# A graph layer's kernel: one more group of rows gathered from x, and another order around the last two groups of edges

## The chip, the cores and the metric

The kernel runs on one core of a Trainium2 chip. The metric is device time in microseconds (us). The engines are TensorE (PE: matmuls; PEld: its weight loads), VectorE (DVE), ScalarE (ACT), GpSimd (POOL) and SyncE (SP). In this kernel POOL issues the gathers (indirect DMAs), and SP nearly all other transfers.

## The reference

N = 6250 nodes with H = 128 features, E = 100000 edges with 4 attributes, the edges sorted by destination:

```python
msg_in = jnp.concatenate([node_features[src], node_features[dst], edge_features], axis=1)
h = jax.nn.silu(msg_in @ mW1 + mb1)
messages = h @ mW2 + mb2
aggregated = jax.ops.segment_sum(messages, dst, num_segments=N)
upd_in = jnp.concatenate([node_features, aggregated], axis=1)
u = jax.nn.silu(upd_in @ uW1 + ub1)
updated = u @ uW2 + ub2
return layer_norm(node_features + updated, ln_g, ln_b)
```

The result is `layernorm(x + that)`, so each node's row is normed twice. All is in float32.

## The kernel before

**Tables.** A product of a gathered row with a weight is the same as a gathered row of the product. So the kernel first forms two tables in device memory: `tab_a` = x times the first 128 rows of `mW1`, and `tab_b` = x times the second 128 rows plus the bias. For that, x is turned tile by tile on TensorE (L339), multiplied (L377), copied out by ACT and DVE (L379, L380) and written by SP (L383, L384), in parts of eight tiles (L367).

**Groups of edges.** The edges go in 98 groups of 1024, each eight tiles of 128 (the last has six). `fetch(g)` (L273) issues eight gathers on POOL, one for each tile, into one of six buffers named `ga`. For groups below `RAW` = 5 it gathers rows of x itself, so that POOL needn't wait for `tab_a`; for the others rows of `tab_a`. Its further arguments are TensorE instructions that the gathers wait for: with two of them, the first holds gather 0 of the group and the second gather 4 (L285 to L294). The groups gathered from x have to be turned (`turn_rows`, L357: eight transposes and a copy back into the buffer) so that `products` can multiply them by the first part of `mW1` (L626). All groups of x are turned while the tables are made. Group 5 is fetched at L404, from `tab_a`, after the turn of group 2.

**The loop** (L680) takes one group in each turn. For group g:

- SP loads the rows of `tab_b` that belong to the group's 96 destinations (`mv`) and the attributes (`st`), four groups ahead (L591, L592).
- `hidden(g)`: DVE adds the gathered rows and the product from PSUM (L640; groups below `RAW` don't need this add), then ACT takes the Silu into `h` (L641).
- `products(g + 2)`: TensorE spreads `tab_b` and the attributes over the edges (L623), and for groups below `RAW` adds the product of the turned rows (L626).
- `node_matrix(g + 3)` (L596) and `edge_matrix(g + 1)` (L609, `oh`) build one-hot matrices on DVE.
- `add(g - 2)` (L665; every fourth group with the counts, L670) adds the sums of an earlier group to `acc`.
- `by_nodes(g)`: TensorE sums `h` over the destinations (L652).
- A fetch: from `CLOSE` = 14 on `fetch(g + 2, begun[g + 2], summing[g])`; that is, gather 0 waits for the first matmul of the group's own products, and gather 4 for the first matmul of the sums of the group now worked on. `products(0)` at L677 stands ahead of the loop, and group 6 takes buffer 0 of the gathers, which `products(0)` reads.

**Nodes.** When the sums of four tiles of nodes are complete, a generator `node_batch` (L466) does the update and both norms, in pieces that end at a `yield`; `advance` (L569) runs one piece of each batch under way, in the loop one a turn, two in turns 92 to 94 and four from turn 95 on (L721). A batch's pieces are: load of its rows `xs`; the products with `u1x`, the fused bias and the sums (L510, L511, L515); Silu to `uT` (L518); the products with `u2` (L521, L530); adding `xs` and the moments (L532, L483, L484); the square root on ACT (L489); scaling (L539 to L546) and second moments; the second root; the shift; the final scaling on ACT (L560); the store by SP. The batch next to last has the tiles from 44 (three tiles) and is started in turn 95. The last batch, `final`, has two tiles and takes its buffers from the gathers' pool.

**After the loop** (L724 to L757) stand what remains of batch 44, the load of `final`'s rows, an activation of one element that brings in the Silu table (L748), the add of group 96, the add and Silu of group 97 in two pieces (L732, L733), its sums, and the rest of `final`.

**Order.** The order on each engine is the order in which the program text issues (`manual_schedule`); each engine's instructions wait on others by semaphores. Two side jobs run as generators too: `destination_checks` (L230), started in turn 2, and `fuse_weights` (L450), started in turn 8. Both use the PSUM tile `y` (`node_y`, L422) that the node batches use, of which there is one.

Of the kernel before, what the change touches and what calls it, by code (L numbers as in the profile page):

```python
# [8 lines left out]
F32 = mybir.dt.float32  # L9
# [9 lines left out]
P = 128  # L19
# [5 lines left out]
def kernel(  # L25
# [40 lines left out]
    nc = tc.nc  # L66
# [5 lines left out]
    G = 8  # L72
# [6 lines left out]
    RB = 14  # L79
    CLOSE = 14  # L80
    LEAD = 4
    RAW = 5
    MADE = 3
    NQ = 4
    NM = 5
# [141 lines left out]
        nc.vector.tensor_copy(base_f, row)  # L227
        nc.vector.tensor_copy(base_i, row)

    def destination_checks(pm):  # L230

        nc.tensor.matmul(pm[:, 0, :NG], ones[0:1, :], base_f, start=True, stop=True)
        yield
        yield
        nc.vector.tensor_scalar(base_p, pm[:, 0, :NG], p_col, None, op0=OP.add)

        far = work.tile([P, 2], F32, name="far", bufs=1)
        nc.vector.tensor_reduce(far[:, 0:1], rel, AX.XY, OP.max)
        nc.vector.tensor_reduce(far[:, 1:2], rel, AX.XY, OP.min)
        mid = (W - 1) / 2  # L240
        nc.vector.tensor_scalar(far, far, -mid, None, op0=OP.add)
        nc.vector.tensor_mul(far, far, far)
        nc.vector.tensor_reduce(far[:, 0:1], far, AX.X, OP.max)
        farthest = work.tile([1, 1], F32, name="farthest", bufs=1)
        yield
        nc.tensor.transpose(pm[0:1, 1, :], far[:, 0:1], ident)
        yield
        yield
        nc.vector.tensor_reduce(farthest, pm[0:1, 1, :], AX.X, OP.max)
        bad = work.tile([1, 2], F32, name="bad", bufs=1)  # L250
        nc.vector.tensor_scalar(bad[:, 0:1], farthest, mid * mid, None, op0=OP.is_gt)

        below = work.tile([1, NG], F32, name="below", bufs=1)
        nc.vector.memset(below, 0.0)
        for i0, n, g in batches[:-1]:
            nc.vector.memset(below[:, g:], float((i0 + n) * P))
        nc.vector.tensor_sub(below, below, base_f)
        nc.vector.tensor_reduce(bad[:, 1:2], below, AX.X, OP.max)
        nc.vector.scalar_tensor_tensor(
            bad_i, bad[:, 1:2], 0.0, bad[:, 0:1], op0=OP.is_gt, op1=OP.max  # L260
        )
# [95 lines left out]
    def turn_rows(g):  # L357
# [4 lines left out]
        nc.vector.tensor_copy(rows[g], px)  # L362
        return ins

    turn_x(*parts[0])
    fetch(1)
    for k, (i0, n) in enumerate(parts):  # L367
# [31 lines left out]
        if k == 4:  # L399
# [1 line left out]
            destinations(0)  # L401
            load_bases(0)
            turn_rows(1)
    fetch(RAW, None, turn_rows(2))  # L404
    for g in range(3, RAW):
        turn_rows(g)
    if E < NG * GE:
        pad = tpool.tile([ED, NG * GE - E], F32, name="pad")
# [13 lines left out]
    def node_y():  # L422
        return node_ps.tile([P, BT, H], F32, name="y")
# [42 lines left out]
    def node_batch(i0, n, work, new, y, final=False):  # L466

        cols = slice(i0 * P, (i0 + n) * P)
        m = (min((i0 + n) * P, N) - i0 * P) // n
        assert m * n == min((i0 + n) * P, N) - i0 * P  # L470

        def rows_of(t):

            return t[i0 * P : i0 * P + m * n].rearrange("(p j) f -> p j f", j=n)

        def flat(t):
            return t[:, :n].rearrange("p i f -> p (i f)")

        def moments(v):
            mv = work.tile([P, BT, 2], F32, name="mv", bufs=2)  # L480
            for i in range(n):
                st = work.tile([P, 6], F32, name="st", bufs=2)
                nc.vector.bn_stats(st, v[:, i, :])  # L483
                nc.vector.bn_aggr(mv[:, i, :], st)  # L484
            return mv

        def std(mv):
            r = work.tile([P, BT], F32, name="r", bufs=2)
            nc.scalar.activation(r[:, :n], mv[:, :n, 1], AF.Sqrt, bias=eps)  # L489
            return r  # L490

        xs = new("xs")
        if m < P:
            nc.vector.memset(xs[m // 32 * 32 :, :n], 0.0)
        nc.sync.dma_start(xs[:m, :n], rows_of(x))
        sums, counts = acc[:, cols], deg[:, cols]
        if not final:

            acc_b, deg_b = new("acc_b"), new("deg_b", DR)
            nc.scalar.copy(flat(acc_b), sums)  # L500
            nc.scalar.copy(flat(deg_b), counts)
            sums, counts = flat(acc_b), flat(deg_b)
        yield
        xb = xs
        if final:
            xb = new("xb")
            nc.vector.tensor_add(xb[:, :n], xs[:, :n], b_b[:, None, :].to_broadcast([P, n, H]))
            nc.vector.tensor_add(xs[:, :n], xs[:, :n], ub2_b[:, None, :].to_broadcast([P, n, H]))
        y = y()
        nc.tensor.matmul(flat(y), u1x, xT[:, cols], start=True, stop=False)  # L510
        nc.tensor.matmul(flat(y), mb2u, counts, start=False, stop=False)  # L511
        if final:

            yield
        nc.tensor.matmul(flat(y), w2u, sums, start=False, stop=True)  # L515
        yield
        uT = new("uT")
        nc.scalar.activation(flat(uT), flat(y), AF.Silu, bias=ub1_col)  # L518
        yield
        if not final:  # L520
            nc.tensor.matmul(  # L521
                y[:, :n],
                ones[0:1, :],
                ub2_row[:, None, :].to_broadcast([1, n, H]),
                start=True,
                stop=False,
            )
        by_p = flat(uT).rearrange("k (p j) -> k p j", j=n)
        for i in range(n):
            nc.tensor.matmul(y[:, i, :], by_p[:, :, i], u2, start=final, stop=final or i == n - 1)  # L530
        yield
        nc.vector.tensor_add(y[:, :n], y[:, :n], xs[:, :n])  # L532
        mv = moments(y)
        if not final:
            nc.vector.tensor_add(xs[:, :n], xs[:, :n], b_b[:, None, :].to_broadcast([P, n, H]))
        yield
        r = std(mv)
        yield
        nc.vector.reciprocal(r[:, :n], r[:, :n])  # L539
        z = new("z")  # L540
        for i in range(n):
            nc.vector.scalar_tensor_tensor(
                y[:, i, :], y[:, i, :], mv[:, i, 0:1], g_b, op0=OP.subtract, op1=OP.mult
            )
            nc.vector.scalar_tensor_tensor(
                z[:, i, :], y[:, i, :], r[:, i : i + 1], xb[:, i, :], op0=OP.mult, op1=OP.add  # L546
            )
        mz = moments(z)
        yield
        rz = std(mz)  # L550
        yield
        nc.vector.reciprocal(rz[:, :n], rz[:, :n])
        shift = work.tile([P, BT], F32, name="shift", bufs=2)
        nc.vector.scalar_tensor_tensor(
            shift[:, :n], mz[:, :n, 0], -1.0, rz[:, :n], op0=OP.mult, op1=OP.mult
        )
        yield
        o = z
        for i in range(n):
            nc.scalar.activation(  # L560
                o[:, i, :], z[:, i, :], AF.Identity, bias=shift[:, i : i + 1], scale=rz[:, i : i + 1]
            )
        yield
        (nc.scalar if final else nc.sync).dma_start(rows_of(out), o[:m, :n])
# [115 lines left out]
    for g in range(NG):  # L680
        if g == 1:
            load_weights()
        if g == 2:
            running.append(destination_checks(node_y()))
        if g == 8:
            running.append(fuse_weights())
        for c in range(1, NC):
            if g == max(1, c * EC // GE - 10):
                attributes(c)
            if g == max(1, c * EC // GE - 10) + 1:  # L690
                attribute_rows(c)
        if g + LEAD < NG:
            load(g + LEAD)
        last = g >= NG - 1
        if not last:
            h[g] = hidden(g)
        if g + 2 < NG:
            pre[g + 2] = products(g + 2)
        if g + MADE < NG:
# [5 lines left out]
        if last:  # L705
            break
        pt[g] = by_nodes(g, h.pop(g), oh.pop(g))
        if CLOSE <= g + 2 < NG:
            fetch(g + 2, begun[g + 2], summing[g])
        elif g == 0:  # L710
            fetch(7, ended[1], begun[2])
        elif g == 1:
            fetch(8, begun[3], summing[1])
        elif g % 2:
            fetch(g // 2 + 8, ended[g + 1], begun[g + 2] if g == CLOSE - 3 else ended[g + 2])
        if g >= NG - 3:
            add(g - 1, pt.pop(g - 1))
        for i0, n, first in batches[:-1]:
            if g == (first if first >= NG - 3 else first + 1):
                running.append(node_batch(i0, n, *node_tiles(nodes, node_y)))  # L720
        for _ in range(4 if g >= NG - 3 else 2 if g >= NG - 6 else 1):  # L721
            advance(running)

    g = NG - 1  # L724
    n = tiles_of(g)
    ga, pg, oh_g, h_g = rows.pop(g), pre.pop(g), oh.pop(g), hbuf[g % NH]
    s = work.tile([P, G, H], F32, name="s")
    primed = consts.tile([1, 1], F32, name="primed")
    before = running.pop()

    def piece(lo, hi):
# [1 line left out]
        nc.scalar.activation(h_g[:, lo:hi], s[:, lo:hi], AF.Silu)  # L733
        sums(g, pt[g], h_g, oh_g, lo, hi)

    final = node_batch(
        *batches[-1][:2],
        nodes,

        lambda name, p=P: gath.tile([P, G, H], F32, name="ga")[:p, :BT],  # L740
        lambda: rows_ps()[:, :BT],
        final=True,
    )
    while running:
        advance(running)
    next(final)

    nc.scalar.activation(primed, ones[0:1, 0:1], AF.Silu)  # L748
    add(g - 1, pt.pop(g - 1))
    pt[g] = degrees(g)  # L750
    next(final)
# [165 lines left out]
```

## Time and profile before

| what | us |
| --- | --- |
| median of 3 runs | 1178.11 (1177.94 to 1178.4) |
| the profiled execution | 1179.78 |
| its span in the trace | 1177.7 |
| mean granted clock of TensorE | 0.668 of full |
| POOL, 782 gathers at 0.95 us and other work | 743.2 busy |

The profile is one execution; its times are compared with its own 1179.78, not with the median. Two rows of the page's groups are for the two kinds of gathers:

```profile
L277 POOL DMA_INDIRECT ga<-tab_a,src_i x742 | 703.7, 948 | 384.2 <-issue 187.1
...
L277 POOL DMA_INDIRECT ga<-in_x_dram,src_i x32 | 30.7, 960 | 16.4 <-issue 8.8
```

A row gives the line, the engine, the operation, output and input, the count, the busy time, the mean in ns, and the idle time just before with what ended most of it. A line of the timeline gives start, duration, engine, line, operation and, in brackets, how long the engine had been idle and what ended that. "issue" is time in which the engine waited for nothing that the profile shows. "remote" means a releaser that the trace couldn't name.

### The profile page before, as it was taken

The numbers are of one execution on the slowest core, as the hardware profiler recorded it, in microseconds if no ns is written. First come the engines' busy times: TensorE is split into PE (matmuls) and PEld (weight loads), VectorE is DVE, ScalarE is ACT, GpSimd is POOL, SyncE is SP. The second block draws the span as 40 slices with busy tenths as digits, with TensorE's granted clock in tenths as the row PEclk, the third lists the DMA queues.
The fourth block names the chain that finished last, engine by engine and source line by source line (L and its number), as shares of the span: only waits on it lengthen the run. The fifth ranks groups of instructions, "written<-read, shape, count | busy, mean of one in ns | idle before, by whom it ended". The sixth has DMA issues, their size and how long they took to land.

```text
span 1177.7 us, 11313 instructions
## 1 busy us (share of the span) xinstructions
PE 747.7 (63%) x3645; PEld 675.3 (57%) x3645; DVE 486.4 (41%) x1017; ACT 238.9 (20%) x297; POOL 743.2 (63%) x790
## 2 busy tenths in 40 slices
PE   5776896656756666567647666656566565656654
PEld 4575786555655656465646565555565464656533
DVE  4461654433532523532533353342343252353344
ACT  2211121220321311120221121121132131122132
POOL 6646666665666666666666666666666666656660
PEclk9877877676565666567566667666666667667665
DMA  8762232222222221222222213221222222212110
GB/s 198 203 156 71 75 85 65 67 82 61 74 66 73 67 72 52 79 72 73 55 72 76 58 57 81 65 81 56 71 74 66 71 74 63 65 55 69 47 59 20
DMA packets 70076, 89.01 MB, mean 76 GB/s; under 512 B 20703, under 2 KB 51694, under 8 KB 70010
## 3 DMA queue, kind: packets, MB, share of 16 engines
q0 software_dynamic: 25024, 51.30, 15.8%
q1 hardware_dynamic: 40408, 35.03, 10.3%
q10 hardware_dynamic: 4578, 1.89, 0.7%
q8 instruction: 31, 0.51, 0.2%
q14 instruction: 35, 0.29, 0.1%
HBM read 76.78 MB, written 11.38 MB: 75 GB/s over the span
## 4 chain that ended last, share of the span: by engine, by line
PE 35%; issue 32%; POOL 20%; DVE 2%; DMA 1%; another core or an unknown queue 1%; ACT 1%; DVEq 0%; POOLq 0%; SPq 0%; ACTq 0%
POOL ga L277 20%; PE pre L623 17%; PE pt L652 14%; PE pre L626 1%; PE y L530 1%; DMA ga<-tab_a,src_i 1%; PE y L521 1%; PE y L510 1%; PE y L511 0%; PE y L515 0%; DVE s L640 0%; DVE st L483 0%; DVE oh L609 0%; PE pt L647 0%
## 5 line engine op out<-in xcount | busy, mean ns | idle before, releaser
L277 POOL DMA_INDIRECT ga<-tab_a,src_i x742 | 703.7, 948 | 384.2 <-issue 187.1
L623 PE MATMUL pre<-mv,st 100*128 100x128 f32 x1564 | 345.1, 396 | 229.5 <-issue 199.5
L623 PEld LDWEIGHTS pre<-mv,st 100*128 100x128 f32 x1564 | 315.2, 301 | 248.4 <-issue 224.3
L652 PE MATMUL pt<-oh,h 128*128 128x96 f32 x1564 | 293.7, 348 | 147.6 <-issue 143.8
L652 PEld LDWEIGHTS pt<-oh,h 128*128 128x128 f32 x1564 | 279.9, 266 | 165.8 <-issue 162.3
L640 DVE TENSOR_TENSOR s<-ga,pre 128x1024 f32<-128x1024 f32 x92 | 112.2, 1220 | 502.6 <-DMA ga<-tab_a,src_i 419.8
L641 ACT ACTIVATE h<-s 128x1024 f32<-128x1024 f32 x92 | 97.1, 1056 | 671.5 <-issue 409.6
L596 DVE TENSOR_SCALAR_CACHE_REDUCE st<-near,p_next 96x1024 f32<-96x1024 uint8 x98 | 124.3, 1270 | 2.9 <-DMA near<-near_d 1.5
L609 DVE TENSOR_TENSOR oh<-w_row,rel 128x768 f32<-128x768 f32 x98 | 93.0, 949 | 42.5 <-remote 42.2
L277 POOL DMA_INDIRECT ga<-in_x_dram,src_i x32 | 30.7, 960 | 16.4 <-issue 8.8
L532 DVE TENSOR_TENSOR y<-y,xs 128x512 f32<-128x512 f32 (+1 forms) x12 | 8.3, 688 | 74.4 <-issue 70.7
L641 ACT ACT_TABLE_LOAD x23 | 29.5, 1283 | 24.2 <-PE pre L626 17.6
L489 ACT ACT_TABLE_LOAD x24 | 30.8, 1283 | 6.1 <-DVE st L483 5.7
L377 PE MATMUL wide<-w,xT 128*128 128x256 f32 x98 | 27.6, 441 | 3.5 <-DVE x_sb L380 3.5
L665 DVE TENSOR_TENSOR acc<-acc,pt 128x96 f32 x98 | 23.7, 242 | 12.5 <-PE pt L652 7.7
L530 PEld LDWEIGHTS y<-u,uT 128*128 128x128 f32 x94 | 22.7, 326 | 10.7 <-issue 10.7
L518 ACT ACTIVATE uT<-y,ub_col 128x512 f32<-128x512 f32 (+1 forms) x12 | 8.1, 678 | 96.5 <-remote 83.6
L377 PEld LDWEIGHTS wide<-w,xT 128*128 128x128 f32 x98 | 21.5, 227 | 8.3 <-DVE x_sb L380 4.3
L530 PE MATMUL y<-u,uT 128*128 128x128 f32 x94 | 25.4, 423 | 0.0
L670 DVE TENSOR_TENSOR deg<-deg,pt 1x96 f32 x98 | 24.4, 249 | 1.0
L626 PE MATMUL pre<-w,ga 128*128 128x128 f32 x80 | 19.4, 326 | 2.7 <-issue 2.6
L521 PE MATMUL y<-ub_row,ones 1*128 1x512 f32 (+1 forms) x24 | 15.5, 729 | 6.9 <-ACT uT L518 6.9
(118 smaller groups left out, 361.7 us busy)
## 6 DMA issues: line engine op xcount, KB each, us to landing
ga<-tab_a,src_i POOLq DMA_INDIRECT x742
near<-near_d SPq DMA_DIRECT2D x24, 384.0 KB
mv<-tab_b SPq DMA_DIRECT2D x98, 48.0 KB
tab_a<-t SPq DMA_DIRECT2D x6, 512.0 KB
tab_b<-x_sb SPq DMA_DIRECT2D x6, 512.0 KB
xs<-in_x_dram SPq DMA_DIRECT2D x11, 256.0 KB
out_dram<-z SPq DMA_DIRECT2D x11, 256.0 KB
st<-ea_d SPq DMA_DIRECT2D x98, 16.0 KB
```

The lines of the kernel that those rows point to most:

```text
L277: ins = nc.gpsimd.indirect_dma_start(out=rows[g][:, i, :], out_offset=None, in_=x if g < RAW else tab_a[:, :], in_offset=bass.IndirectOffs ...
L377: ins = nc.tensor.matmul(pm[:, j], xT[:, cols], w1, start=True, stop=True)
L489: nc.scalar.activation(r[:, :n], mv[:, :n, 1], AF.Sqrt, bias=eps)
L521: nc.tensor.matmul(y[:, :n], ones[0:1, :], ub2_row[:, None, :].to_broadcast([1, n, H]), start=True, stop=False,)
L530: nc.tensor.matmul(y[:, i, :], by_p[:, :, i], u2, start=final, stop=final or i == n - 1)
L596: nc.vector.tensor_scalar(stbuf[g % NST][:W], near.pop(g), p_next, 0.0, op0=OP.is_equal, op1=OP.add, accum_out=deg_q[g // DQ % 2][:, g % D ...
L609: nc.vector.tensor_tensor(oh, w_row[:, None, :].to_broadcast([P, G, W]), rel[:, g, :, None].to_broadcast([P, G, W]), op=OP.is_equal,)
L623: ins = nc.tensor.matmul(pre[:, i, :], st[:, i, :], mv[g % NM], start=True, stop=g >= RAW)
L626: ins = nc.tensor.matmul(pre[:, i, :], rows[g][:, i, :], w1[:, 0, :], start=False, stop=True)
L640: nc.vector.tensor_add(s[:, :n], ga[:, :n], ps[:, :n])
L641: nc.scalar.activation(h[:, :n], s[:, :n], AF.Silu)
L652: ins = nc.tensor.matmul(pt[:, :W], h[:, i, :], oh[:, i, :], start=i == 0, stop=i == tiles_of(g) - 1)
```

## The change

- `RAW` is 6: group 5 is gathered from x too. Its fetch, still after the turn of group 2, waits for no table.
- Group 5 is not turned beside the tables but in the loop, by a new generator `turn_late`: in two halves, each of four transposes into the PSUM tile `y` and a copy back by DVE, advanced in turns 1 to 3. `products(5)` then has eight L626 products, and `hidden(5)` has no add.
- `destination_checks` starts in turn 7 instead of 2, takes its own PSUM tile and has two yields less; `fuse_weights` starts in turn 4 instead of 8.
- In turn 96 the four advances of batch 44 stand at the head of the turn, ahead of `hidden(96)`, and none at its end.
- `fetch(97)` has no waits for TensorE; those of the groups from 14 to 96 stay.
- `final` is created, and its rows loaded, at the end of turn 95; its next piece (the two adds to `xs` and the product with `u1x`) stands at the end of turn 96, and a new yield parts that product from the one with the bias, which needs the last counts.
- The activation that brought in the Silu table ahead of the last group is gone.

```diff
-    RAW = 5
+    RAW = 6
...
-    def destination_checks(pm):
+    def destination_checks():
...
+        pm = node_y()
         nc.tensor.matmul(pm[:, 0, :NG], ones[0:1, :], base_f, start=True, stop=True)
-        yield
         yield
...
+    def turn_late(g):
+
+        for lo in range(0, G, BT):
+            px = node_y()
+            for i in range(BT):
+                nc.tensor.transpose(px[:, i, :], rows[g][:, lo + i, :], ident)
+            yield
+            nc.vector.tensor_copy(rows[g][:, lo : lo + BT], px)
...
-    fetch(RAW, None, turn_rows(2))
-    for g in range(3, RAW):
+    fetch(RAW - 1, None, turn_rows(2))
+    for g in range(3, RAW - 1):
         turn_rows(g)
...
         nc.tensor.matmul(flat(y), u1x, xT[:, cols], start=True, stop=False)
+        if final:
+
+            yield
         nc.tensor.matmul(flat(y), mb2u, counts, start=False, stop=False)
...
-        if g == 2:
-            running.append(destination_checks(node_y()))
-        if g == 8:
+        if g == 4:
             running.append(fuse_weights())
+        if g == 7:
+            running.append(destination_checks())
...
+        if g == NG - 2:
+
+            for _ in range(4):
+                advance(running)
         if not last:
             h[g] = hidden(g)
+        if g == 1:
+            late = turn_late(RAW - 1)
+        if 1 <= g <= 3:
+            next(late, None)
...
-        if CLOSE <= g + 2 < NG:
+        if CLOSE <= g + 2 < NG - 1:
             fetch(g + 2, begun[g + 2], summing[g])
+        elif g + 2 == NG - 1:
+            fetch(g + 2)
...
-        for _ in range(4 if g >= NG - 3 else 2 if g >= NG - 6 else 1):
+        for _ in range(0 if g == NG - 2 else 4 if g == NG - 3 else 2 if g >= NG - 6 else 1):
             advance(running)
+        if g == NG - 3:
+            final = node_batch(
...
+            next(final)
+        if g == NG - 2:
+            next(final)
...
-    primed = consts.tile([1, 1], F32, name="primed")
...
-    next(final)
-
-    nc.scalar.activation(primed, ones[0:1, 0:1], AF.Silu)
     add(g - 1, pt.pop(g - 1))
     pt[g] = degrees(g)
     next(final)
```

More of the change, by code (lines that the diff above doesn't have):

```diff
@@ L246, in destination_checks @@
         nc.tensor.transpose(pm[0:1, 1, :], far[:, 0:1], ident)
-        yield
         yield
@@ L720 @@
                 running.append(node_batch(i0, n, *node_tiles(nodes, node_y)))
-        for _ in range(4 if g >= NG - 3 else 2 if g >= NG - 6 else 1):
+        for _ in range(0 if g == NG - 2 else 4 if g == NG - 3 else 2 if g >= NG - 6 else 1):
             advance(running)
+        if g == NG - 3:
+            final = node_batch(
+                *batches[-1][:2],
+                nodes,
+                lambda name, p=P: gath.tile([P, G, H], F32, name="ga")[:p, :BT],
+                lambda: rows_ps()[:, :BT],
+                final=True,
+            )
+            next(final)
+        if g == NG - 2:
+            next(final)
     g = NG - 1
@@ L734, in piece @@
         sums(g, pt[g], h_g, oh_g, lo, hi)
[L736 to L743, printed above, removed]
     while running:
         advance(running)
-    next(final)
-    nc.scalar.activation(primed, ones[0:1, 0:1], AF.Silu)
     add(g - 1, pt.pop(g - 1))
```

## The prediction, made before the changed kernel was run

> **What bounds the kernel now.** I read the page first (engine shares, the chain), then the waits of GpSimd, then the timeline at three places: the start of the gathers, one turn of the steady state, the last 50 us.
>
> ```profile
> PE 747.7 (63%) x3645; PEld 675.3 (57%) x3645; DVE 486.4 (41%) x1017; ACT 238.9 (20%) x297; POOL 743.2 (63%) x790
> PE 35%; issue 32%; POOL 20%; DVE 2%; DMA 1%; another core or an unknown queue 1%; ACT 1%; DVEq 0%; POOLq 0%; SPq 0%; ACTq 0%
> ...
> POOL ga L277 <- issue: 198.1, 648, 0.6
> POOL ga L277 <- remote: 141.4, 48, 3.6
> ...
> POOL ga L277 <- DMA tab_a<-t: 9.8, 1, 9.8
> ```
>
> No engine is full. POOL issues 782 gathers; each takes 0.95 us and is followed by 0.30 us of issue, so a gather costs 1.25 us and all of them 977 us of a span of 1177.7. The rest is stops: 48 of about 3 us called "remote", and one of 9.8 us near the start.
>
> ```profile
> 1058.88 0.95 POOL L277 DMA_INDIRECT ga<-tab_a,src_i  x1 [3.42 <-remote]
> ...
> 1082.04 0.95 POOL L277 DMA_INDIRECT ga<-tab_a,src_i  x1 [3.45 <-remote]
> ...
> 1105.17 0.94 POOL L277 DMA_INDIRECT ga<-tab_a,src_i  x1 [3.43 <-remote]
> ```
>
> A stop comes every 23.2 us: 16 gathers (20 us) and some 3.3 us. So the loop has a fixed beat, and what shifts its start or comes after its last gather moves the end one for one. Those two places are what the change touches.
>
> ```profile
> 69.88 0.94 POOL L277 DMA_INDIRECT ga<-tab_a,src_i  x1 [9.79 <-DMA tab_a<-t]
> 73.39 0.76 PE L623 MATMUL pre<-mv,st 100*128 100x128 f32 x2 [7.32 <-DMA st<-ea_d]
> 81.62 0.94 POOL L277 DMA_INDIRECT ga<-tab_a,src_i  x1 [2.06 <-PE pre L626]
> 104.92 0.94 POOL L277 DMA_INDIRECT ga<-tab_a,src_i  x1 [3.61 <-remote]
> ```
>
> The first of these is group 5, waiting for the table; the third is group 6, waiting for the last matmul of products(0), which frees buffer 0 of the six; the fourth is group 8.
>
> ```profile
> 1138.92 1.22 DVE L640 TENSOR_TENSOR s<-ga,pre 128x1024 f32<-128x1024 f32 x1 [2.77 <-DMA ga<-tab_a,src_i]
> 1145.82 0.94 POOL L277 DMA_INDIRECT ga<-tab_a,src_i  x1 [2.46 <-remote]
> 1145.87 0.58 ACT L518 ACTIVATE uT<-y,ub_col 128x384 f32<-128x384 f32 x1 [7.50 <-remote]
> 1147.07 0.95 POOL L277 DMA_INDIRECT ga<-tab_a,src_i  x1 [0.30 <-issue]
> ```
>
> This is the end of the loop: the add of group 96, the held gather of group 97, the Silu of node batch 44, the last gather. From the chain of waits over the last 50 us:
>
> ```profile
> 1149.82 0.58 DVE y L532
> ...
> 1155.48 0.09 DVE mv L484
> ...
> 1156.08 2.08 DMA ga<-in_x_dram
> 1158.25 0.44 DVE ga L507
> ...
> 1159.17 0.70 DVE s L732
> ```
>
> The chain runs through DVE's norm of batch 44, then through the xs load of the final batch, to the add of group 97. From 1159.17 to the end it is 18.5 us in one line.
>
> **What the Trainium skill says.** "Perfetto Trace Analysis", Tensor Engine Instruction: the end that a trace gives for a matmul is modelled, while DVE, ACT and GpSimd run strictly first in, first out. The trace agrees with the order: DVE idles 2.77 us ahead of the add of group 96 and nothing overtakes it; and L515 of batch 44 is shown over at 1139.61 while its reader starts at 1145.87. "ScalarE: Activation LUTs", What ACT_TABLE_LOAD costs: a load takes about 1283 ns and a drain may follow it; here the load's mean is 1283 and no drain shows. "TensorE: Matmul & The Clock Gate", Part 1: TensorE has half its clock until some 3.4 us of work have gone by; here the 16 matmuls of sums(96) take 3.62 us at a granted clock of 0.5.
>
> **The change part by part.**
>
> *Group 5 from x.* Its eight gathers need no table any more: they follow group 4 (last one over at 60.1) and the turn of group 2, so they fall into the stretch from 60.1 to 69.9, where POOL is idle. That removes the 9.79 us stop and the eight gathers behind it (69.88 to 79.57). But what is late next is group 6: it waits for products(0), which begins at 73.39 on a load that follows the tables and runs 16 pairs of matmuls to about 81.4. Nothing in the change starts that sooner. So group 6 stays at about 81.6, and of the 9.8 us nothing reaches the beat. Bounds: −1.3 us if products(0) runs a little sooner with no gathers beside it, and +2.6 us if the gathers slow the tables: 8 gathers of 65.6 KB (51.3 MB over 782) are 0.52 MB, 2.6 us at the 203 GB/s that this core moves from 60 to 70, where the DMA engines are already 71% busy. I take +0.5.
>
> *Group 5 turned in the loop.* It adds 8 transposes (0.33 us each at L361 in the trace's model, nearer 0.12 in a row: 24 in 2.78 us), so 0.9 us, at half clock 2; 8 L626 matmuls of two passes, 16 × 0.12, 1.9 us; two DVE copies of 128x512 at about 0.65 less one L640 of 1.22. DVE comes out even (+0.1), and in that stretch is busy 7 of 12 us. TensorE gets about 3 us, and it is not idle there: in the six stretches of 12 us from 105 to 177 the table of windows gives 10.74, 9.90, 12.00, 8.30, 10.57 and 10.55 (mean 10.3). Gathers of groups 8 to 13 wait for TensorE's products, so this may all count (+3) or vanish in POOL's stops of 2 to 3.6 us (0). I take half, +1.5. The checks moved from group 2 to 7 and the fused weights from 8 to 4 have the same instructions; the checks wait less, which I cost at nothing because DVE idles 5 of 12 us there; if a TensorE result is waited for in DVE's queue it is up to +0.5, inside the bounds.
>
> *Batch 44 ahead of the rows of group 96.* DVE now has in this order: L532 of batch 44 and its moments, scaling and second moments; the add of group 96; oh(97); add(95); the two xb adds; add(96) and its counts; the add of group 97. Before, the add of group 96 was over at 1140.14. With uT where it was, L532 starts at 1149.82 and the norm ends at 1155.66 as before; then the group's add, 1.22, to 1156.9. ACT loads Silu again after the second Sqrt (1156.06 + 1.28 = 1157.34), then h(96), 1.06, to 1158.4; sums(96) 3.62 to 1162.0; add(96) 0.26 and counts 0.50, some 1.0 with their issue; the add of group 97 at 1163.0 against 1159.17. That is +3.85. The oh(97), add(95) and xb adds (0.95 + 0.26 + 0.86) lie beside h and sums. If sums(96) ran at full clock (1.9 us, as 16 of L652 do in the loop) it would be +2.1: lower bound.
>
> *Final xs load early, no priming.* SP's load is now issued at group 95, behind the store of batch 40 and ahead of the store of batch 44; it waits for a memset of 0.28 on DVE and the old readers of its buffer, and nothing urgent is behind it. The 2.08 us of the chain on it, the two xb adds and L748's 1.28 go. But this is no second gain: in the new order the add of group 97 waits for sums(96), and the 1163.0 is already counted without them.
>
> *Last gathers without waits.* Group 97 lost its stops of 1.33 and 2.46. POOL could end at 1144.3 to 1144.8, not 1148.0. Group 97's rows were long there at 1159.17, so nothing is gained from them directly. But L515's result came out at 1145.87, within 0.1 us of POOL's restart at 1145.82 and of a DVE add held 4.80 us at 1145.80; in the loop, too, TensorE's results come in bursts when POOL resumes (h(2) held for 16.87 us until 104.45, group 8's restart being 104.92). I read that gathers in flight hold them back. If POOL runs through to 1144.8 and the release comes a stop's length (2.5 to 3.5) later, uT is at 1147.3 to 1148.3, +1.5 to +2.5; if a stop falls as before, 0; if the waits removed were what held it, L515 shows at 1139.7 and it is −6. I take +0.3 of a step that most likely is 0 to +1.5.
>
> Sum against the profiled execution: +0.5 + 1.5 + 3.85 + 0.3 = +6.1 us. That execution took 1179.78 (span 1177.7 and 2.1 around it), so 1185.9 there; it lies 1.67 above the median of 1178.11, so the forecast is 1178.1 + 6.1 = 1184.2.
>
> **The rivals.**
>
> *As before.* TensorE's 3 us vanish in POOL's stops, the head is even, sums(96) runs warm: +2.1, and uT a little sooner by −1 to −2 as POOL ends 3 us sooner: 1178 to 1179. For it: the loop's beat has slack on every engine. Against: the clock has been at 0.5 from 1140.8 on, and with TensorE waiting longer there it has no reason to rise.
>
> *Faster, the other side.* The waits of group 97 were what held L515's result. Then uT is at 1139.7, L530 over at 1143.5, the norm at 1149.4, the add of group 96 at 1150.6, h to 1152.1 (Silu already loaded by then), sums to 1155.7, the add of group 97 at 1156.5: −2.7, with head and TensorE's work near nothing 1175.2. It decides when uT comes more than some 4 us sooner, before 1142. For it: three engines released together with POOL's held gather. Against: the same bursts appear at every stop in the loop, where POOL waits and TensorE is slow too.
>
> *Slower at the head.* Gathers from 60 to 70 hold back the turns of groups 2 to 4 and the tables: +2.6 instead of +0.5, and TensorE's work at its full 3: 1188. For it: 71% busy DMA engines there; against: three earlier groups gathered beside the tables cost no visible stall.
>
> That the 9.8 us are gained whole would need group 6 sooner; the buffer excludes it.
>
> **How the numbers follow.** Forecast (slower) 0.62, as before 0.14, faster 0.16, slower at the head 0.08. The likeliest alone: low bounds 0 + 0 + 2.1 + 0 above 1178.1 to 1.3 + 3 + 3.85 + 1.5, so 1180.5 to 1188. For 8 in 10 the range goes from 1175.0, which takes in half of the faster case, to 1189.0. This kernel can be told from no change by about 0.2%, 2.4 us: faster 0.16, same 0.14, slower 0.70.
>
> **What would show it.** Right: POOL idle from about 70 to 81.6 instead of 60 to 70, group 6 at 81 to 83; the steady beat 23.2; the add of group 96 at 1156 or later; the add of group 97 about 4 us later than before against POOL's last gather of the beat; uT within 2 us of where it was. Wrong: group 6 well before 80 (then the head gained), or uT soon after L515 and the add of group 97 before 1159.

## The result, and the profile after

The changed kernel takes 1185.77 us (median of 6 runs, 1185.51 to 1187.96) against 1178.26 us (6 runs, 1176.51 to 1179.82): 1.0069 times as long, 95% interval 1.0056 to 1.0082, that is some 6.6 to 9.7 us slower. Its profiled execution took 1185.51, with a span of 1183.7, 6.0 more than the span before.

The start of the gathers, from the timeline of POOL after (line numbers are those of the changed kernel: the gathers are L276, `products` L634 and L637, `hidden` L651 and L652, `by_nodes` L663):

```profile
67.15 0.95 POOL L276 DMA_INDIRECT ga<-in_x_dram,src_i  x1 [1.99 <-remote]
...
70.89 0.95 POOL L276 DMA_INDIRECT ga<-in_x_dram,src_i  x1 [0.31 <-issue]
...
80.54 0.95 POOL L276 DMA_INDIRECT ga<-tab_a,src_i  x1 [8.70 <-PE pre L637]
...
105.05 0.95 POOL L276 DMA_INDIRECT ga<-tab_a,src_i  x1 [4.81 <-PE pre L634]
...
1104.93 0.95 POOL L276 DMA_INDIRECT ga<-tab_a,src_i  x1 [3.45 <-remote]
```

Group 5 is fetched by 71.8, and the wait for the table is gone. In its place stands one of 8.70 us, for the last product of group 0, which frees the buffer of group 6. Group 6 begins 1.08 us sooner than before (80.54 against 81.62), group 8 already 0.13 us later (105.05 against 104.92), and group 94, the last whole beat, 0.24 us sooner (1104.93 against 1105.17). The long loop in between gave or took next to nothing. So the loss lies in the last 80 us.

The 1.08 us don't come from products of group 0 that ran sooner. Here is the last of them, first in the kernel before, then in the changed one:

```profile
79.62 0.39 PE L626 MATMUL pre<-w,ga 128*128 128x128 f32 x2
...
79.88 0.39 PE L637 MATMUL pre<-w,ga 128*128 128x128 f32 x2
```

In the changed kernel these products begin 1.26 us later (74.65 against 73.39) and are shown over 0.26 us later (80.27 against 80.01). But POOL starts 0.27 us after that end, where in the kernel before, with group 5's last gather begun at 78.63, it started 1.61 us after it.

The last 50 us, from the timeline of all engines after:

```profile
1140.21 0.80 PE L526 MATMUL y<-acc_b,w2u 128*128 128x384 f32 x1 [1.64 <-issue]
...
1143.63 0.95 POOL L276 DMA_INDIRECT ga<-tab_a,src_i  x1 [0.30 <-issue]
1148.24 0.58 ACT L529 ACTIVATE uT<-y,ub_col 128x384 f32<-128x384 f32 x1 [10.18 <-remote]
...
1158.23 1.22 DVE L651 TENSOR_TENSOR s<-ga,pre 128x1024 f32<-128x1024 f32 x1 [0.19 <-issue]
...
1159.74 1.06 ACT L652 ACTIVATE h<-s 128x1024 f32<-128x1024 f32 x1
...
1160.85 3.73 PE L663 MATMUL pt<-oh,h 128*128 128x96 f32 x16 [8.60 <-ACT h L652]
...
1164.62 0.26 DVE L676 TENSOR_TENSOR acc<-acc,pt 128x96 f32 x1 [3.34 <-PE pt L663]
...
1165.32 0.69 DVE L764 TENSOR_TENSOR s<-ga,pre 128x512 f32<-128x512 f32 x1
```

The last line is the add of group 97. POOL issues its last gather at 1143.63 (1147.07 before), after 18 gathers without a stop. The product that uT needs, L526, is shown over at 1141.01, yet uT starts 7.23 us after that. It comes 2.37 us later than before (1148.24 against 1145.87), and 2.61 later against the beat at group 94. From uT to the add of group 97 it is 17.08 us, before 13.30: 3.78 more, and in it stand, one after another, the add of group 96, its Silu, its 16 sums and their add, as the new order has them. From that add to the end it is 18.4 us against 18.5. The account of the two spans is −0.24 + 2.61 + 3.78 − 0.15 = +6.0.

### The profile page after: what moved, and what is told of

Same layout as the page of the kernel before. It is cut to its first block, busy times and chain, and to the rows that moved or that the text cites. A ratio compares the mean times of both kernels' runs of the same rounds, so it can differ in the third digit from the quotient of the medians.

```text
span 1183.7 us, 11354 instructions
## 1 busy us (share of the span) xinstructions
PE 729.9 (62%) x3669; PEld 665.9 (56%) x3669; DVE 486.3 (41%) x1018; ACT 239.0 (20%) x296; POOL 743.1 (63%) x790
## 5 line engine op out<-in xcount | busy, mean ns | idle before, releaser
L276 POOL DMA_INDIRECT ga<-tab_a,src_i x734 | 696.3, 949 | 376.5 <-issue 194.4
L634 PE MATMUL pre<-mv,st 100*128 100x128 f32 x1564 | 334.9, 387 | 233.2 <-issue 211.8
L634 PEld LDWEIGHTS pre<-mv,st 100*128 100x128 f32 x1564 | 307.8, 294 | 250.6 <-issue 237.2
L663 PE MATMUL pt<-oh,h 128*128 128x96 f32 x1564 | 291.2, 345 | 167.2 <-issue 156.3
L663 PEld LDWEIGHTS pt<-oh,h 128*128 128x128 f32 x1564 | 278.9, 263 | 183.1 <-issue 172.6
L651 DVE TENSOR_TENSOR s<-ga,pre 128x1024 f32<-128x1024 f32 x91 | 111.0, 1220 | 494.1 <-DMA ga<-tab_a,src_i 428.2
L652 ACT ACTIVATE h<-s 128x1024 f32<-128x1024 f32 x91 | 96.1, 1056 | 652.7 <-issue 419.9
L276 POOL DMA_INDIRECT ga<-in_x_dram,src_i x40 | 38.0, 949 | 20.8 <-issue 11.0
L385 PE MATMUL wide<-w,xT 128*128 128x256 f32 x98 | 24.2, 403 | 1.0 <-DVE x_sb L388 0.9
L637 PE MATMUL pre<-w,ga 128*128 128x128 f32 x96 | 21.1, 304 | 0.4 <-issue 0.4
```

The costliest lines, as they stand in the source:

```text
L276: ins = nc.gpsimd.indirect_dma_start(out=rows[g][:, i, :], out_offset=None, in_=x if g < RAW else tab_a[:, :], in_offset=bass.IndirectOffs ...
L385: ins = nc.tensor.matmul(pm[:, j], xT[:, cols], w1, start=True, stop=True)
L634: ins = nc.tensor.matmul(pre[:, i, :], st[:, i, :], mv[g % NM], start=True, stop=g >= RAW)
L651: nc.vector.tensor_add(s[:, :n], ga[:, :n], ps[:, :n])
L652: nc.scalar.activation(h[:, :n], s[:, :n], AF.Silu)
L663: ins = nc.tensor.matmul(pt[:, :W], h[:, i, :], oh[:, i, :], start=i == 0, stop=i == tiles_of(g) - 1)
```

## The experiments

Times of different chips differ here, so each run is told as a ratio to the kernel before on the same chip. There were two kinds of chip, and that turned out to matter: on one the kernel before takes 1169 us, and POOL stops after every 16 gathers in the steady part of the loop, as in the profile before; on four others it takes 1013 us, and in the runs made there POOL doesn't stop in the loop (d_wait_sum and e_wait_sum have one stop, of 1.36 and 0.72 us, at the wait that they add). In short "with stops" and "without stops". The result above is from a chip with stops too (1178 us). Of the kernel before only that one profile exists, so where the timeline of a run with stops is set beside "before", the two can be of different chips.

| run | chip | ratio (95%) | us against before |
| --- | --- | --- | --- |
| a_batch_back | without | 0.9971 (0.9961 to 0.9982) | −2.9 |
| a_waits_back | without | 1.0021 (1.0013 to 1.0030) | +2.1 |
| a_both_back | without | 0.9981 (0.9973 to 0.9989) | −1.9 |
| b_rows_only | without | 1.0002 (0.9994 to 1.0010) | +0.2 |
| b_batch_ahead | with | 1.0038 (1.0027 to 1.0048) | +4.4 |
| b_no_waits | with | 1.0019 (1.0011 to 1.0026) | +2.2 |
| c_wait_sum_both | with | 1.0052 (1.0034 to 1.0070) | +6.1 |
| c_wait_sum_after | with | 1.0080 (1.0055 to 1.0106) | +9.4 |
| d_wait_sum | without | 0.9969 (0.9959 to 0.9979) | −3.1 |
| d_both_back | without | 0.9967 (0.9955 to 0.9980) | −3.3 |
| e_wait_sum | without | 0.9976 (0.9968 to 0.9983) | −2.4 |
| d_after | without | 1.0023 (1.0015 to 1.0032) | +2.3 |

The last column is the ratio less one, times the median of the kernel before on that chip.

### The order around group 96, alone

```diff
+        if g == NG - 2:
+            for _ in range(4):
+                advance(running)
         if not last:
             h[g] = hidden(g)
...
-        for _ in range(4 if g >= NG - 3 else 2 if g >= NG - 6 else 1):
+        for _ in range(0 if g == NG - 2 else 4 if g == NG - 3 else 2 if g >= NG - 6 else 1):
```

The kernel before with this edit (b_batch_ahead).

> The kernel before with only batch 44's pieces moved ahead of the add of group 96. My theory: +3.8 us, less or more by what the late load of the last rows (2.1 us on the chain before) now hides behind the sums of group 96: 1181 to 1183. Rival (the order is no cost of its own): 1178.

Measured: +4.4 us (3.2 to 5.6), on a chip with stops. The timeline of its tail:

```profile
1134.76 0.58 ACT L518 ACTIVATE uT<-y,ub_col 128x384 f32<-128x384 f32 x1 [8.10 <-remote]
...
1144.75 1.22 DVE L640 TENSOR_TENSOR s<-ga,pre 128x1024 f32<-128x1024 f32 x1 [0.19 <-issue]
...
1147.38 3.73 PE L652 MATMUL pt<-oh,h 128*128 128x96 f32 x16 [8.60 <-ACT h L641]
...
1152.76 1.02 DVE L736 TENSOR_TENSOR s<-ga,pre 128x512 f32<-128x512 f32 x2
```

From uT to the add of group 97 it is 18.00 us, against 13.30 in the kernel before. That is 4.7 (4.8 against the 13.21 of the run below, which has the old order on the same chip), more than the 3.78 of the changed kernel, since here the two adds to the last rows (0.42 each) stand behind the counts of group 96, and there ahead of them. The order is a cost of its own.

### The waits of group 97, alone

```diff
-        if CLOSE <= g + 2 < NG:
+        if CLOSE <= g + 2 < NG - 1:
             fetch(g + 2, begun[g + 2], summing[g])
+        elif g + 2 == NG - 1:
+            fetch(g + 2)
```

The kernel before with this edit (b_no_waits).

> The kernel before with only the waits of group 97 taken away. My theory (gathers in flight hold back what TensorE reports): POOL ends at about 1144.6, uT some 3.5 us after its last gather begins, at 1147.5 to 1148.5; +2.4 us, about 1180.6. Rival (the waits of POOL themselves held TensorE's result): uT soon after 1140, and 4 to 6 us faster. Second rival: no change.

Measured: +2.2 us (1.3 to 3.0), on the same chip. The timeline of its tail:

```profile
1094.96 0.94 POOL L277 DMA_INDIRECT ga<-tab_a,src_i  x1 [3.31 <-remote]
...
1130.58 0.48 PE L515 MATMUL y<-acc_b,w2u 128*128 128x384 f32 x1 [3.02 <-issue]
...
1133.41 0.94 POOL L277 DMA_INDIRECT ga<-tab_a,src_i  x1 [0.30 <-issue]
1137.85 0.25 DVE L665 TENSOR_TENSOR acc<-acc,pt 128x96 f32 x1 [7.17 <-remote]
1137.92 0.58 ACT L518 ACTIVATE uT<-y,ub_col 128x384 f32<-128x384 f32 x1 [10.86 <-remote]
```

The first line is group 94's first gather, so uT comes 42.96 us after the beat, against 40.70 before: +2.26, the whole measured loss. (In b_batch_ahead, which has the waits and ran on the same chip, it comes after 40.24.) The product that uT needs is shown over at 1131.06, the last gather begins at 1133.41, and uT and a waiting add of DVE start together 4.5 us after that (3.5 was expected). The rival, that POOL's own waits held the result, is out: with them gone it came later. The waits are worth 2.2 us on this chip. That gathers in flight are what holds the result fits, but this run can't tell it from a delay of TensorE's own: between the two halves of L515 TensorE itself sits idle for 3.02 us, for which the trace names nothing.

The two runs together make 6.6 us, the low end of the changed kernel's 6.6 to 9.7.

### The same wait elsewhere, and eight gathers too many

These two put one wait into POOL's queue, on the product that uT needs (L526 in the changed kernel), behind the advances of turn 95:

```diff
-        elif g + 2 == NG - 1:
-            fetch(g + 2)
...
+        if g == NG - 3:
+            fetch(NG - 1, summed[batches[-2][0]])
```

c_wait_sum_both has batch 44's pieces at the end of turn 96, c_wait_sum_after ahead of group 96's add.

> The changed kernel with batch 44's pieces back at the end of turn 96, and with gather 0 of group 97 waiting for the last product of batch 44 (one wait, no other), its issue standing behind that product. If gathers in flight hold back TensorE's results, this stops POOL at about 1137.3 and lets the product be seen at once: POOL restarts and uT starts at about 1140 to 1141, some 5 us sooner than in the kernel before; the add of group 97 at 1151 to 1153, and the time about 1171. Rival (the result is late for a reason of TensorE's own): uT stays at 1145 to 1146 and POOL is held until then, the last gather comes at 1153, and the time is 1178 or more.

> The changed kernel (batch 44 ahead of group 96's add) with the same wait of gather 0 of group 97 on batch 44's last product. If uT comes at 1140 to 1141, the norm ends at about 1150.5, the add of group 96 at 1151.9, sums to 1157, the add of group 97 at about 1158: 1177 to 1178.5, which is 5 to 7 us more than with the pieces at the end of the turn. Rival: with an early uT the changed order pays, and this is the faster of the two.

Measured: +6.1 and +9.4 us. Neither tests what it was made for. With the two lines at the top gone, the next branch of that `elif` chain fetches group 55 once more in turn 95, eight gathers ahead of those of group 97, into a buffer that nobody reads (798 instructions on POOL, not 790). In c_wait_sum_both POOL stops at the second wait of those gathers, and uT comes 0.7 us after its restart, 40.78 us after the beat: its old place. In c_wait_sum_after that wait cost no stop, so that 16 gathers ran on end:

```profile
1129.86 0.81 PE L526 MATMUL y<-acc_b,w2u 128*128 128x384 f32 x2
...
1140.11 0.94 POOL L276 DMA_INDIRECT ga<-tab_a,src_i  x1 [0.30 <-issue]
1142.63 0.58 ACT L529 ACTIVATE uT<-y,ub_col 128x384 f32<-128x384 f32 x1 [15.48 <-remote]
1142.80 0.94 POOL L276 DMA_INDIRECT ga<-tab_a,src_i  x1 [1.75 <-remote]
```

The product is shown over at 1130.67 and uT starts at 1142.63, 12 us later and 2.5 us after the last gather of the run began. Eight gathers began between the product and uT here, three in the changed kernel, where the hold was 7.2 us. So the hold is no fixed delay of TensorE; in both it ends when POOL's run of gathers has ended, as the theory says. This came by accident, in one trace. The order's part is unsettled by the pair: 1.0080 and 1.0052 have intervals that overlap.

### Parts of the changed kernel put back

a_batch_back moves the four advances back to the end of turn 96 (the first diff above, reversed), a_waits_back puts the waits back (the second, reversed), a_both_back does both.

> The changed kernel with batch 44's four pieces of turn 96 back at the end of that turn, as in the kernel before. My theory (the order costs 3.8 us in the tail, and the early load of the last rows then shows a gain of some 1.6 us that the order had hidden): about 5 us faster than the changed kernel, 1180 to 1181; the add of group 96 near 1141 and that of group 97 some 1.9 us after the norm of batch 44 ends. Rival (the loss is TensorE's added work at the start): 1184 to 1186 as the changed kernel.

> The changed kernel with the two waits of the gathers of group 97 put back. My theory (with POOL running on, the result of batch 44's last product is seen 2.4 us later): uT back at about 1145.8 and 2.4 us faster than the changed kernel, about 1183.3. Rival (uT comes late for another reason, as the order of the last loads): no change, 1185.8, uT at 1148.

> The changed kernel with both put back; of the change there stay the six groups from x, the early load of the last rows and the missing table load. My theory: the two add up, about 7.5 us faster than the changed kernel, 1177 to 1178.5, that is 0 to 1.5 us faster than the kernel before. Rival (TensorE's added work or the head costs): 1179.5 to 1182.

These came on a chip without stops, on which the predicted times mean nothing; the ratios do. With the order put back the kernel is faster than before by 2.9 us. With only the waits put back it is slower by 2.1, hence the order costs 4.0 there (1.0021 less 0.9981 of 1012.8). The waits make no difference that shows: 0.9971 without, 0.9981 with, in the old order, and the intervals overlap. What a_waits_back was made to test, the waits on a chip with stops, it couldn't. The timeline of a_batch_back shows both why the waits don't matter there and what the early load brings:

```profile
978.91 0.81 PE L526 MATMUL y<-acc_b,w2u 128*128 128x384 f32 x2
979.53 0.94 POOL L276 DMA_INDIRECT ga<-tab_a,src_i  x1 [0.30 <-issue]
979.82 0.58 ACT L529 ACTIVATE uT<-y,ub_col 128x384 f32<-128x384 f32 x1 [3.73 <-PE y L526]
...
988.42 0.18 DVE L492 BATCH_NORM_AGGREGATE mv<-st 128x2 f32<-128x6 f32 x1
988.52 0.39 DVE L515 TENSOR_TENSOR ga<-ga,b_b 128x256 f32<-128x256 f32 x1
988.94 0.42 DVE L516 TENSOR_TENSOR ga<-ga,ub_b 128x256 f32<-128x256 f32 x1
...
989.98 1.02 DVE L760 TENSOR_TENSOR s<-ga,pre 128x512 f32<-128x512 f32 x2
```

uT starts 0.10 us after its product, with gathers on both sides of it: nothing is held back. And the add of group 97 starts 1.38 us after batch 44's norm (988.60).

### The rows, alone

The kernel before with `RAW` = 6, `turn_late` and the two moved side jobs (b_rows_only).

> The kernel before with only the first part of the change: six groups from x, the sixth turned in the loop, the two side jobs moved. My theory (group 6 waits for products(0) as before, and what is gained or lost at the start is taken up by the beat): within 1 us of the kernel before, group 6 at about 80.5, group 94 within 0.5 us of 1105. Rivals: TensorE's added work of about 3 us shows, up to +3; or the 9.8 us stop was worth something, -1.3 or more.

Measured: 1.0002 (0.9994 to 1.0010), +0.2 us, on the chip without stops. There group 6 waits 5.06 us for the products of group 0. It still has the late load, and its timeline is the counterpart of the last fence:

```profile
988.00 0.18 DVE L492 BATCH_NORM_AGGREGATE mv<-st 128x2 f32<-128x6 f32 x1
...
988.29 0.27 DVE L502 MEMSET ga<- 32x256 f32 x1
...
990.71 0.43 DVE L515 TENSOR_TENSOR ga<-ga,b_b 128x256 f32<-128x256 f32 x1 [1.45 <-DMA ga<-in_x_dram]
991.17 0.42 DVE L516 TENSOR_TENSOR ga<-ga,ub_b 128x256 f32<-128x256 f32 x1
991.63 0.69 DVE L744 TENSOR_TENSOR s<-ga,pre 128x512 f32<-128x512 f32 x1
```

3.45 us from the norm's end (988.18) to the add of group 97, against 1.38: the early load is worth 2.1 us where the order doesn't cover it. The rows alone were not run on a chip with stops, and the expected places of groups 6 and 94 hold for such a chip alone; there only the beat in the trace of the changed kernel speaks for them.

### What was left: the changed kernel elsewhere, and a version that is faster

d_wait_sum is c_wait_sum_both without the eight gathers, e_wait_sum the same kernel again, d_both_back is a_both_back again, and d_after the changed kernel.

> As c_wait_sum_both, but without the eight gathers that that kernel issued once too often: the changed kernel with batch 44's pieces at the end of turn 96, and gather 0 of group 97 waiting for the last product of batch 44. On a chip where POOL stops after every 16 gathers: with the result held back by gathers in flight, POOL stops at its end of group 96 and uT comes some 2.5 to 3.5 us after that, 3 to 5 us sooner than in the kernel before; with the 1.9 us of the early load, 5 to 7 us faster than the kernel before (ratio 0.994 to 0.996). Rival (the result is late for a reason of TensorE's own): uT at its old place, ratio 0.998 or more. On a chip where POOL doesn't stop: the product is seen at once anyway, POOL loses up to 2 us that nothing needs, ratio 0.997 to 0.998 as a_batch_back.

> a_both_back once more, for a chip where POOL stops after every 16 gathers: of the change there stay the six groups from x, the early load of the last rows and the missing table load. Theory: 1.5 to 2.5 us faster than the kernel before (ratio 0.998 to 0.9987), uT at its place of before, the add of group 97 1.4 to 1.6 us after batch 44's norm. Rival (TensorE's added work at the start, or the head): ratio 1.000 to 1.003.

> d_wait_sum once more, for a chip where POOL stops after every 16 gathers; the expectation is that of d_wait_sum for such a chip: uT 3 to 5 us sooner than in the kernel before relative to POOL's last beat, ratio 0.994 to 0.996; the rival 0.998 or more. If the chip doesn't stop: 0.997 again.

> The changed kernel itself once more, beside a_batch_back and a_waits_back. If the chip is one where POOL doesn't stop: the missing waits can't delay uT there, so only the order is left, less the early load: 2 to 3 us slower than the kernel before (ratio 1.002 to 1.003), uT within 0.2 us of the end of its product. If it is one that stops: 1.006 to 1.007, uT about 3.5 us after POOL's last gather begins. Rival for both (the waits cost by themselves, with or without stops): the same ratio of about 1.007 on either chip.

All four came on chips without stops. So d_wait_sum and e_wait_sum answer only what was said for such a chip, and d_both_back nothing that its expectation asked: they are 2.4 to 3.3 us faster than the kernel before, whether gather 0 waits for L526 or the two waits of before are there. The test planned for the theory, on a chip with stops, was not made. d_after decides more; its uT:

```profile
978.61 0.81 PE L526 MATMUL y<-acc_b,w2u 128*128 128x384 f32 x2
979.23 0.94 POOL L276 DMA_INDIRECT ga<-tab_a,src_i  x1 [0.30 <-POOLq L795]
979.51 0.58 ACT L529 ACTIVATE uT<-y,ub_col 128x384 f32<-128x384 f32 x1 [2.48 <-PE y L526]
```

uT starts 0.09 us after its product, and the changed kernel loses only 2.3 us (1.5 to 3.2), where it lost 6.6 to 9.7 with stops. With the waits put back it loses 2.1 (a_waits_back). So the missing waits cost nothing by themselves; they cost on a chip with stops, where b_no_waits has them at 2.2 us.

Of the versions here, the changed kernel with batch 44's pieces back at the end of turn 96 beats both kernels on the chips without stops (0.9967 to 0.9981, with the waits and without). On a chip with stops it wasn't run, but for c_wait_sum_both with its eight gathers too many.

## Why the prediction was right

The direction, the range and the largest step, the order, held: +6.1 was said, the medians differ by 7.5 and the spans by 6.0. That the sum came so near is in part luck, since two terms were off by over 2 us in opposite ways. Point by point:

- *The wait of group 5 is replaced by that of group 6* for products(0): as said, 80.54 in the trace, within the bounds; +0.5 was taken, and what is left of it at group 94 is −0.24 together with TensorE's work. The reason given for an earlier group 6, products(0) running sooner, was not what happened: they began later and ended later, and only POOL's start followed their end more closely. The trace of before has that end at 80.01, not at the 81.4 that I read. The other end of the bound, 2.6 us for slower tables, did not come; of the 1.26 us by which the products began later, 0.26 was left at their end.
- *TensorE's added work, +1.5*: too much. From group 6 to group 8 a lead of 1.08 us turned into a lag of 0.13. That TensorE's work took these 1.2 us is likely but not shown; by the steady beat they were gone, and together with the head it was +0.2 us (−0.6 to +1.0) on the chip without stops. As far as the beat shows, the lower of my two bounds was right.
- *The order, +3.85*: 3.78 in the trace of the changed kernel, 4.4 by itself with the late load still in the kernel, 4.0 on a chip without stops. sums(96) took 3.73 us, not the 1.9 of a full clock, as taken.
- *The early load is no second gain in the new order*: right, and a_batch_back beside b_rows_only gives its worth without that order, 2.1 us.
- *Waits taken away, +0.3*: this is the mis-sized term. I had named +1.5 to +2.5 as the case in which POOL runs through and the release comes a stop's length after it, and took the other end as likelier. It was +2.4 in the trace (+2.6 against the beat) and +2.2 alone. The reason given for it, gathers that hold TensorE's results back, fits the holds with stops (6.3 us before, 7.2 after, 12 with more gathers on end); why nothing is held without stops, where the gathers run on too, it doesn't say.
- The errors of these terms (about +2.2 on the start and TensorE, −2.3 on the waits) cancel. The sum was better than its parts.
- *The signs named*: POOL's idle stretch, the beat (23.2) and the add of group 96 (1158.23) came as said, and group 6 half a microsecond ahead of its 81 to 83. Two missed: uT was to lie within 2 us of its old place and came 2.4 later, and the add of group 97 was to come about 4 us later against the beat and came 6.4 later. In both the excess is the term of the waits.

The rival on the faster side (POOL's waits themselves held uT) is refuted by b_no_waits. The rival "as before" had the start right, and sums(96) at full clock and an earlier uT wrong. What holds a result back while gathers run on, and why only on some chips, the traces don't tell: they call it "remote".

## What to carry to other kernels

A wait that is removed is worth what the next one behind it leaves: here a buffer took over 8.7 of 9.8 us. An engine's queue in program order makes a late chain later for all that stands behind it, so put work whose inputs are there ahead of work that waits, not the other way round; and look at the end of a kernel by itself, where each step on the chain counts whole. Where stops in the profile have no named cause, find out whether another chip has them before an order is tuned around them.

## What the runs showed of the hardware that was not expected

- The same program takes 1169 to 1178 us where POOL stops and 1013 us on four other chips. The changed kernel was profiled on both kinds, with spans of 1183.7 and 1011.9 us. Of the difference of 171.8, 147.6 lie between the start of group 6 and the last gather: there POOL has 52 stops, of 159.6 us in all, on the one chip, and no wait of more than 0.3 us on the other. A gather takes about the same time (0.95 and 0.94 us).
- In these two profiles TensorE too is idle with no cause named ("issue") for 375.9 us with stops and for 40.6 without. So with stops the delay shows on TensorE itself and not only in those who wait for its results; which comes first isn't shown.
- With stops, at the end of the loop, a TensorE result that was shown over late in a run of gathers was seen by ACT and DVE only 2.5 to 4.6 us after the last gather of a run on POOL began (4.6 in the changed kernel, 4.5 in b_no_waits, 2.5 in c_wait_sum_after). On chips without stops it was seen within 0.1 us.
- But gathers in flight alone don't hold a result. Early in a run on POOL it is seen at once with stops too, as here in the kernel before, in the fifth and sixth gathers after the stop that ends at 1105.17:

```profile
1109.16 2.24 PE L530 MATMUL y<-u,uT 128*128 128x128 f32 x8
1110.17 0.95 POOL L277 DMA_INDIRECT ga<-tab_a,src_i  x1 [0.30 <-issue]
...
1111.43 0.95 POOL L277 DMA_INDIRECT ga<-tab_a,src_i  x1 [0.30 <-issue]
1111.50 0.70 DVE L532 TENSOR_TENSOR y<-y,xs 128x512 f32<-128x512 f32 x1 [4.67 <-issue]
```

The products are shown over at 1111.40, and DVE's add starts 0.10 us later.
